# Another order of the convolution units, with the keys' lower half last, on one NeuronCore

## Chip, cores and metric

The kernel runs on 1 core of one Trainium2 chip. The metric is the device time of one execution in microseconds. The kernel before took 4063.36 us (median of 3 runs, 4057.63 to 4075.92). A change of 0.5% of that is 20 us.

## What is computed

An image of 64 x 64 positions with 256 channels goes through two layers. The first is a hybrid of convolutions and attention; the second is a bidirectional state-space scan and a mixture of experts. All is in float32. The change touches the first layer only as far as the attention's inputs (and one step of the layer norm inside the attention phase):

```python
qkv = concat([conv(xc, W1, 0), conv(xc, W3, 1), conv(xc, W5, 2)])   # q: 1x1, k: 3x3, v: 5x5
qkv = conv(qkv, Wdw, 1, groups=3 * c)                               # depthwise 3x3
q, k, v = split(qkv, 3); q, k = l2n(q), l2n(k)                      # per head and position
attn = softmax(einsum('bhnc,bhmc->bhnm', q, k) * temperature)       # 8 heads, 4096 positions
o = conv(einsum('bhnm,bhmc->bhnc', attn, v), Wproj, 0);  x = x + o
```

## The kernel before

**Units.** `conv_phase` cuts the three convolutions into 12 units `(kind, half, t)`: kind q, k or v; half 0 (upper) or 1 (lower) of the picture; t one of the two groups of 128 output channels. This text writes k00 for `("k", 0, 0)`, v01 for `("v", 0, 1)`, and so on. The 3x3 and 5x5 convolutions are done in Winograd form along the rows: a k unit has 6 jobs (points), a v unit has 8; a job is one accumulated product of transformed weights and transformed inputs in a PSUM bank (L465). A q unit is four plain 1x1 products (L457).

**Stages of a unit.** For k and v, `transform_out` combines the jobs' results in pairs on VectorE (`out_t`, `pad`, L289 and L286; one of a pair is first copied by ScalarE, L494) and writes the convolution's rows into one of two tiles `pad`, used in turn (`pads[n % 2]`). `sides` (ScalarE, L518, L519) fills the columns at the margins. Then `depthwise` makes the 3x3 depthwise convolution of `pad` in two pieces: a first tap on ScalarE (L557), one tap by ScalarE and an accumulating DMA (L562, L563), and 15 taps on VectorE (L570; 768 values a row for half 0, 1280 for half 1). Of v, the result is turned by TensorE (`turn`, L637, copied by ScalarE, L639) and stored to `vd`. Of q and k, three chunks of 512 positions at a time are normalised: squares on ScalarE (L600), sums on TensorE (L601), inverse root on ScalarE (L608 to L610), spread on TensorE (L615), product on VectorE (L289 `acc<-acc,ps`), for q a copy on ScalarE (L624), and a store (L628).

**Halves.** The depthwise convolution of the lower half needs 9 rows of the upper half; they are kept in `edge` tiles in SBUF, copied by ScalarE (L795, L757). k and v of the same t use one `edge` tile.

**Fills.** What the jobs need is also made on VectorE: `all_weights` transforms weights (v: 15 steps of about 1.9 us for each t) and sends them to DRAM, from which the SP queue loads them again (L443); `inputs` makes the transformed inputs of a kind and half (v: about 32 us). Nine `place` buffers hold these inputs. The list `fills` sets their order, `step_fill` takes the next step.

**Order.** Inside `tc.manual_schedule` each engine runs its instructions in the order in which the program emits them. While unit n's jobs run on TensorE, its groups call `step(main)` (output transform), `feed()` (jobs, as far as their weights and inputs have been emitted; at most 3 not yet used, 4 PSUM banks), `tick()` (due norm stages), `step(before)` (depthwise of unit n-1), `step_fill()`. So the order in the VectorE and TensorE queues is fixed at build time, and an engine whose next instruction must wait does nothing else.

```python
units = [("k", h, t) for h in range(2) for t in range(CT)]
units += [("q", 0, 0), ("v", 0, 0), ("q", 0, 1), ("v", 0, 1), ("q", 1, 0), ("v", 1, 0), ("q", 1, 1), ("v", 1, 1)]
```

**End of the phase.** Of the last unit (v11), 16 of 40 rows are made by TensorE: `diagonal` puts the nine taps on diagonals, `products` (L533) multiplies `pad` by them. `attention_phase` then loads q, keys and values (L935, L916, L917) into SBUF that the convolution phase used; these loads are queued on SP behind the end of that phase. Its first score product is L1048.

Of the kernel before, what the change touches and what calls it, by code (L numbers as in the profile page):

```python
# [24 lines left out]
P = 128  # L25
# [3 lines left out]
CT = C // P  # L29
# [32 lines left out]
def step(gen, n=1):  # L62

    for _ in range(n):
        if gen is None or next(gen, StopIteration) is StopIteration:
            return False
    return True
# [115 lines left out]
def conv_phase(cx, xT, w1, w3, w5, temp, qd, kd, vd, uk, uv):  # L183
# [13 lines left out]
    nc, tc = cx.nc, cx.tc  # L197
    HR = 32
    LAG = 24
    TX = W // 4  # L200
    with ExitStack() as ctx:
        one = ctx.enter_context(tc.tile_pool(name="a_one", bufs=1))
# [24 lines left out]
        for pad in pads:  # L227
# [2 lines left out]
        edges = {  # L230
            k: one.tile([P, 9, 4, TX], FP, name=f"edge{i}") for i, k in enumerate((0, 1, ("q", 0), ("q", 1)))
        }
        out_t = one.tile([P, 4 * N], FP, name="out_t")
        wq = one.tile([P, CT, C], FP, name="wq")
        for t in range(CT):
# [187 lines left out]

        units = [("k", h, t) for h in range(2) for t in range(CT)]
        units += [("q", 0, 0), ("v", 0, 0), ("q", 0, 1), ("v", 0, 1), ("q", 1, 0), ("v", 1, 0), ("q", 1, 1), ("v", 1, 1)]
        jobs = [
            (u, i) for u in units for i in (range(4) if u[0] == "q" else PTS[u[0]])
        ]  # L430
# [90 lines left out]
        spare = one.tile([P, (H - LAG) * W // 2], FP, name="spare")  # L521
        diag = spare[:, 0 : 9 * P].rearrange("p (a b) -> p a b", b=P)

        def diagonal(ch):
            for tap in range(9):
                w_ap = wdw[:, 9 * ch + tap : 9 * ch + tap + 1]
                nc.scalar.activation(diag[:, tap, :], cx.ident, AF.Copy, scale=w_ap)

        def products(pad, r, ps):

            for tap in range(9):
                dy, dx = divmod(tap, 3)
                nc.tensor.matmul(  # L533
                    ps.rearrange("p (h s j) -> p h s j", s=4, j=TX), diag[:, tap, :],
                    pad[:, r + dy : r + dy + 8, dx : dx + 4, :], start=tap == 0, stop=tap == 8,
                )

        def depthwise(kind, half, t, pad):

            row0, n = (LAG, H - LAG) if half else (0, LAG)  # L540
            ch = {"q": 0, "k": CT, "v": 2 * CT}[kind] + t
            dst = accp.tile([P, (H - LAG) * W], FP, name="acc", tag="acc")
            shared = 16 if (kind, half, t) == units[-1] else 0
            mine = n - shared

            def piece(b, tap):
                dy, dx = divmod(tap, 3)
                m = mine // 2
                return (
                    dst[:, m * W * b : m * W * (b + 1)].rearrange("p (h w) -> p h w", w=W),  # L550
                    pad[:, m * b + dy : m * b + dy + m, dx : dx + 4, :].rearrange("p h s j -> p h (s j)"),
                    wdw[:, 9 * ch + tap : 9 * ch + tap + 1],
                )

            for b in range(2):
                o, src, w_ap = piece(b, 0)
                nc.scalar.activation(o, src, AF.Copy, scale=w_ap)  # L557
            away = (kind, half, t) not in units[-2:]
            if away:
                o, src, w_ap = piece(1, 8)  # L560
                x = spare[:, 0 : mine * W // 2]
                nc.scalar.activation(x.rearrange("p (h w) -> p h w", w=W), src, AF.Copy, scale=w_ap)  # L562
                nc.gpsimd.dma_start(out=dst[:, mine * W // 2 : mine * W], in_=x, accum_op=ALU.add)  # L563
            parts = [pcv.tile([P, N], FP, name="cv", tag="cv") for _ in range(shared // 8)]
            for i, ps in enumerate(parts):
                products(pad, mine + 8 * i, ps)
            for b in range(2):
                for tap in range(1, 8 if b and away else 9):
                    o, src, w_ap = piece(b, tap)
                    nc.vector.scalar_tensor_tensor(o, src, w_ap, o, ALU.mult, ALU.add)  # L570
                    yield
                if kind == "v":
                    m = mine * W // P // 2
                    turn(dst, t, row0 * W // P, m * b, m)
                if b == 0 and shared:
                    for i, ps in enumerate(parts):
                        nc.scalar.copy(dst[:, W * (mine + 8 * i) : W * (mine + 8 * i + 8)], ps)
                    turn(dst, t, row0 * W // P, 2 * m, shared * W // P)
            if kind != "v":
                c0 = row0 // ROWS  # L580
                rows_left.extend((dst[:, N * j : N * j + N], kind, t, c0 + j) for j in range(n // ROWS))
                if not busy and (kind, half, t) == units[-2]:
                    norm_sums()
                elif not busy:
                    busy.append(None)
                    later(norm_sums)
# [68 lines left out]
        with tc.manual_schedule(engines=ORDERED):  # L655
# [56 lines left out]
            def all_weights(kind, co):  # L712
# [5 lines left out]
                ready.add((kind, co))  # L718

            fills = [  # L720
                first, all_weights("k", 1), inputs("k", 1),
                all_weights("v", 0), inputs("v", 0),
                all_weights("v", 1), inputs("v", 1),
            ]

            pure = fills[1::2]

            second = fills[5]

            def step_fill():  # L730

# [20 lines left out]
            before = None  # L752
            for n, (kind, half, t) in enumerate(units):
                pad, r0 = pads[n % 2], 9 if half else 1
                edge = edges[(kind, t) if kind == "q" else t]
                if half:
                    nc.scalar.copy(pad[:, 0:9, 1:5, :], edge)  # L757
                    nc.gpsimd.memset(pad[:, HR + 9, :, :], 0.0)
                else:
                    nc.gpsimd.memset(pad[:, 0, :, :], 0.0)  # L760
                if kind == "q":
                    def evacuate():
                        for i in range(4):
                            r = r0 + 16 * (i // 2)
                            nc.scalar.copy(
                                pad[:, r : r + 16, 1 + 2 * (i % 2) : 3 + 2 * (i % 2), :],
                                product().rearrange("p (h s j) -> p h s j", s=2, j=TX),
                            )
                        sides(pad, r0)
                        yield  # L770

                    main, groups = evacuate(), 1
                else:
                    main, groups = transform_out(kind, pad, r0), len(PTS[kind]) // 2
                if n == 0:
                    feed()
                    for _ in range(6):
                        step_fill()
                for g in range(groups):
                    step(main)  # L780
                    feed()
                    tick()

                    for _ in range(12 if kind == "q" else 0):
                        step_fill()

                    for _ in range(9 if n == len(units) - 1 else -(-18 // groups)):
                        step(before)
                    for _ in range(share[kind]):
                        step_fill()  # L790
                    feed()
                drain(main)
                drain(before)
                if not half:
                    nc.scalar.copy(edge, pad[:, LAG : LAG + 9, 1:5, :])  # L795
                before = depthwise(kind, half, t, pad)
                if n == len(units) - 2:
                    diagonal(2 * CT + units[-1][2])

            left = True  # L800
            while left or events:
                tick()
                for _ in range(4):
                    left = left and step(before)

# [79 lines left out]
def attention_phase(cx, early, xT, wproj, qd, kd, vd, x1d, ud):  # L887
# [8 lines left out]
    with ExitStack() as ctx:  # L896
# [41 lines left out]
        def project(c, oT):  # L938

            xr = tl.tile([P, CT, N], FP, name="xr", tag="xr")  # L940
            nc.sync.dma_start(out=xr, in_=xT[:, N * c : N * c + N].rearrange("(t p) n -> p t n", p=P))
            yield
            x1 = tl.tile([P, CT, N], FP, name="x1", tag="x1")
            for co in range(CT):
                ps = aside()
                for t in range(CT):
                    nc.tensor.matmul(
                        ps, wpj[:, t, P * co : P * co + P], oT[:, t, :], start=t == 0, stop=t == CT - 1
                    )
                yield  # L950
                nc.vector.tensor_tensor(x1[:, co, :], xr[:, co, :], ps, ALU.add)
                yield
            nc.sync.dma_start(out=x1d[c], in_=x1)
            if c == NCH - 1:
                return
            u = tl.tile([P, CT, N], FP, name="u", tag="xr")
            yield from layer_norm(cx, tl, aside, x1, u, None, 1, halves=True)
            nc.sync.dma_start(out=ud[c], in_=u)
            yield

# [1456 lines left out]
```

## Time and profile before

| | us |
|---|---|
| median of 3 runs (lowest, highest) | 4063.36 (4057.63, 4075.92) |
| the profiled execution | 4052.57, span 4050.8 |
| first convolution product on TensorE starts | 37.83 |
| first product of a v unit starts | 211.76 |
| last convolution product (L465) and the norm products after it end | 566.7 |
| q load of the attention issued on SP | 604.02 |
| first attention score product starts | 611.56 |

The profile comes from one execution. Engines: PE is TensorE, DVE is VectorE, ACT is ScalarE, POOL is GpSimd, SP issues DMAs. In a timeline a row is "start, duration, engine, line, operation, output<-input, shapes, count", and in brackets the idle time before it with what ended it; PE lists two entries for each product of the program. In the table by windows the columns are the window, its length, each engine's busy time with its count of instructions, the granted clock of TensorE, the DMA share and GB/s.

### The profile page before, as it was taken

What the parts mean: (1) busy time and instruction counts of PE and PEld (TensorE: products, weight loads), DVE (VectorE), ACT (ScalarE), POOL (GpSimd) and SP (SyncE); (2) the same over time, 40 slices, a digit from 0 to 9 for tenths busy, and PEclk for the clock granted to TensorE, in tenths of its full rate; (3) what the DMA queues carried; (4) which work ended last, traced back from release to release, by engine and by line L of the source; (5) the groups of instructions that cost most, each with busy time, mean ns of one, the idle gap of its engine ahead of it and who ended that gap; (6) DMA issues with size and microseconds to landing.
All of it is one profiled execution on the core that took longest, in us unless ns stands there. A gap on an engine that the chain in (4) does not pass through costs nothing. (4 is left out here: it accounts for less than half of the span.)

```text
span 4050.8 us, 43236 instructions
## 1 busy us (share of the span) xinstructions
PE 3566.8 (88%) x14792; PEld 1173.0 (29%) x14792; DVE 3441.4 (85%) x2887; ACT 2656.2 (66%) x4152; POOL 1849.2 (46%) x1294
## 2 busy tenths in 40 slices
PE   6789989999999999997888888888888888886898
PEld 2333432222222222222222222222222222222444
DVE  8997668988988888778899999999999999999322
ACT  1123238887887888775777777777787777775222
POOL 3120010000000000013888899898898989987100
PEclk9889989999999999998888898999899899988999
DMA  6342315232232332224343344243434444432111
GB/s 215 105 134 93 100 63 154 53 74 53 64 69 51 66 67 53 51 53 150 105 122 115 111 123 144 99 146 116 129 109 122 127 126 121 135 108 94 63 62 56
DMA packets 165763, 404.91 MB, mean 100 GB/s; under 512 B 37157, under 2 KB 46629, under 8 KB 165278
## 3 DMA queue, kind: packets, MB, share of 16 engines
q1 hardware_dynamic: 137166, 304.26, 24.3%
q0 software_dynamic: 26064, 89.42, 9.5%
q10 hardware_dynamic: 2304, 8.39, 0.6%
q8 instruction: 118, 1.93, 0.2%
q14 instruction: 111, 0.91, 0.1%
HBM read 268.17 MB, written 79.56 MB: 86 GB/s over the span
## 5 line engine op out<-in xcount | busy, mean ns | idle before, releaser
L1907 POOL TENSOR_TENSOR dbx<-dtxr,b 128x1024 f32<-128x1024 f32 x512 | 1202.8, 2359 | 190.5 <-DVE da L1920 89.8
L1055 ACT ACTIVATE e<-sc 128x1024 f32<-128x1024 f32 x1024 | 993.9, 1023 | 183.3 <-PE sc L1048 153.5
L1920 DVE TENSOR_TENSOR_SCAN da<-da,state,dbx 128x1024 f32<-128x1024 f32 x432 | 1014.1, 2347 | 20.2 <-POOL dbx L1907 6.3
L965 DVE TENSOR_TENSOR s<-s,e 128x1024 f32<-128x1024 f32 x768 | 880.2, 1219 | 17.6 <-ACT e L1055 17.0
L1897 ACT ACTIVATE da<-dtr,aneg 128x512 f32<-128x512 f32 x1024 | 708.1, 692 | 33.9 <-DMA dtr<-dtd 3.3
L1048 PE MATMUL sc<-q,kS 32*128 32x512 f32 x4096 | 650.3, 646 | 17.0 <-ACT e L1055 12.9
L1925 DVE TENSOR_TENSOR h<-da,c 128x1024 f32<-128x1024 f32 x432 | 529.2, 1225 | 33.2 <-DVE da L1920 1.4
L972 PE MATMUL av<-e,vT 128*32 128x512 f32 x4096 | 555.0, 608 | 0.3 <-ACT e L1055 0.3
L988 POOL DMA_DIRECT2D s<-s x94 | 81.5, 880 | 943.7 <-DVE s L965 850.3
L1960 PE MATMUL y<-h,sel 128*32 128x512 f32 x2048 | 372.2, 659 | 92.0 <-DVE h L1925 67.6
L465 PE MATMUL cv<-v,u 128*128 128x512 f32 x928 | 414.2, 607 | 42.6 <-DVE out_t L289 15.6
L1048 PEld LDWEIGHTS sc<-q,kS 32*128 32x128 f32 x4096 | 212.0, 184 | 458.6 <-issue 246.8
L1353 PE MATMUL mm<-u,win 128*128 128x512 f32 x464 | 245.3, 670 | 64.5 <-ACT z L1461 28.2
L1951 ACT COPY state<-da 128x2 f32<-128x2 f32 x431 | 68.8, 160 | 293.6 <-DVE h L1925 290.8
L570 DVE SCALAR_TENSOR_TENSOR acc<-pad,wdw_s,acc 128x768 f32<-128x768 f32 (+1 forms) x182 | 224.7, 1240 | 42.5 <-ACT acc L557 37.1
L465 PEld LDWEIGHTS cv<-v,u 128*128 128x128 f32 x928 | 179.5, 195 | 273.8 <-issue 226.7
L143 POOL TENSOR_TENSOR ln_few<-ln_few,minus_half 128x4 f32<-128x4 f32 x29 | 38.4, 1325 | 399.1 <-DMA ln_few<-ln_row 235.7
L1399 PE MATMUL mm<-xp,taps 128*128 128x512 f32 x480 | 213.3, 596 | 0.1
L965 DVE TENSOR_TENSOR s<-e 128x1024 f32<-128x1024 f32 x128 | 151.9, 1218 | 58.1 <-ACT e L1055 57.9
L1920 DVE TENSOR_TENSOR_SCAN h<-da,state,dbx 128x1024 f32<-128x1024 f32 x80 | 187.5, 2344 | 12.5 <-ACT state L1951 9.8
L972 PEld LDWEIGHTS av<-e,vT 128*32 128x32 f32 x4096 | 82.2, 108 | 397.7 <-issue 386.9
L1930 POOL TENSOR_TENSOR h<-h,c 128x1024 f32<-128x1024 f32 x80 | 188.4, 2355 | 1.0 <-ACT state L1951 1.0
(379 smaller groups left out, 3859.2 us busy)
## 6 DMA issues: line engine op xcount, KB each, us to landing
dtr<-dtd SPq DMA_DIRECT2D x128, 512.0 KB
dtxr<-dtd SPq DMA_DIRECT2D x128, 512.0 KB
s<-s POOLq DMA_DIRECT2D x94, 512.0 KB, 5.8
b<-bcd SPq DMA_DIRECT2D x64, 256.0 KB
c<-bcd SPq DMA_DIRECT2D x64, 256.0 KB
dtd<-dt SPq DMA_DIRECT2D x64, 256.0 KB
dtd<-few SPq DMA_DIRECT2D x64, 256.0 KB
u<-uv SPq DMA_DIRECT2D x24, 640.0 KB
```

The source lines that it names most:

```text
L465: nc.tensor.matmul(rows4(ps), u[:, dy, P * ci : P * ci + P], v[:, dy : dy + HR, ci, :], start=dy + ci == 0, stop=dy == k - 1 and ci == CT - 1,
L570: nc.vector.scalar_tensor_tensor(o, src, w_ap, o, ALU.mult, ALU.add)
L965: nc.vector.tensor_tensor(z, x, y, ALU.add)
L972: nc.tensor.matmul(g.av[32 * h : 32 * h + 32, :], vT[:, kb, P * t + 32 * h : P * t + 32 * h + 32], es[h // 2][:, h % 2, :], start=kb == 0, ...
L1048: nc.tensor.matmul(ps[h // 2][:, h % 2, :], kS[r, t, P * kb : P * kb + P], q_t[r, t, :], start=True, stop=True,)
L1055: nc.scalar.activation(e, ps[i], AF.Exp)
L1353: nc.tensor.matmul(ps, win[d][:, t, P * e : P * e + P], u[:, t, ::-1] if d else u[:, t, :], start=t == 0, stop=t == CT - 1,)
L1897: nc.scalar.activation(da[:, v, :], dts[i, e, j][0][:, v, :], AF.Exp, scale=aneg[i % 2][:, a : a + 1])
L1907: nc.gpsimd.tensor_tensor(u, dts[i, e, j][1], bcs[i, k][0][:, None, :].to_broadcast([P, 2, N]), ALU.mult)
L1920: nc.vector.tensor_tensor_scan(das[n].rearrange("p v n -> p (v n)"), da.rearrange("p v n -> p (v n)"), u.rearrange("p v n -> p (v n)"), st ...
L1925: nc.vector.tensor_tensor(h, da, bcs[i, k][1][:, None, :].to_broadcast([P, 2, N]), ALU.mult)
L1960: nc.tensor.matmul(ys[i, e][32 * j : 32 * j + 32, :], cx.sel, hs[n + j // 2][:, j % 2, :], start=False, stop=k == SQ - 1,)
```

## The change

The units come in another order: k00, k01, v00, q00, v01, q01, v10, q10, v11, q11, k10, k11. The fills follow: after the keys' weights come the values' weights and inputs, and the inputs for the keys' lower half are last. Since k and v are no longer finished one after the other, the 9 rows of k go through DRAM (`k_edges`, a store and a load on the SP queue for each t) instead of an `edge` tile. The last unit is now k11. Its 16 rows on TensorE are dealt out among the VectorE taps (`products` has become a generator), its first taps are emitted ahead of the due norm stages (`left = step(before)` before the loop), and in the last unit's groups after the first `feed()` and `tick()` are called once more. In the attention phase the layer norm of chunk 6 gets one more step of distance (`rest` 2).

```diff
+    SHARED = 1
+        k_edges = [cx.rows.tile([P, 9, 4, TX], FP, name=f"k_edge{t}", tag=f"k_edge{t}") for t in range(CT)]
...
-        units = [("k", h, t) for h in range(2) for t in range(CT)]
-        units += [("q", 0, 0), ("v", 0, 0), ("q", 0, 1), ("v", 0, 1), ("q", 1, 0), ("v", 1, 0), ("q", 1, 1), ("v", 1, 1)]
+        units = [
+            ("k", 0, 0), ("k", 0, 1), ("v", 0, 0), ("q", 0, 0), ("v", 0, 1), ("q", 0, 1),
+            ("v", 1, 0), ("q", 1, 0), ("v", 1, 1), ("q", 1, 1), ("k", 1, 0), ("k", 1, 1),
+        ]
...
                     pad[:, r + dy : r + dy + 8, dx : dx + 4, :], start=tap == 0, stop=tap == 8,
                 )
+                yield
...
-            shared = 16 if (kind, half, t) == units[-1] else 0
+            shared = 16 if (kind, half, t) in units[-SHARED:] else 0
-            away = (kind, half, t) not in units[-2:]
+            away = (kind, half, t) not in units[-SHARED - 1 :]
...
-            for i, ps in enumerate(parts):
-                products(pad, mine + 8 * i, ps)
+            beside = [products(pad, mine + 8 * i, ps) for i, ps in enumerate(parts)]
+            yield
             for b in range(2):
                 for tap in range(1, 8 if b and away else 9):
                     o, src, w_ap = piece(b, tap)
                     nc.vector.scalar_tensor_tensor(o, src, w_ap, o, ALU.mult, ALU.add)
+                    for _ in range(3 if beside else 0):
+                        if beside and not step(beside[0]):
+                            beside.pop(0)
                     yield
...
+                while beside:
+                    drain(beside.pop(0))
...
             fills = [
-                first, all_weights("k", 1), inputs("k", 1),
-                all_weights("v", 0), inputs("v", 0),
-                all_weights("v", 1), inputs("v", 1),
+                first, all_weights("k", 1), all_weights("v", 0), inputs("v", 0),
+                all_weights("v", 1), inputs("v", 1), inputs("k", 1),
             ]
-            pure = fills[1::2]
-            second = fills[5]
+            pure = [fills[1], fills[2], fills[4]]
+            second = fills[4]
...
                 if half:
-                    nc.scalar.copy(pad[:, 0:9, 1:5, :], edge)
+                    if kind == "k":
+                        nc.sync.dma_start(out=pad[:, 0:9, 1:5, :], in_=k_edges[t])
+                    else:
+                        nc.scalar.copy(pad[:, 0:9, 1:5, :], edge)
...
+                    if n == len(units) - 1 and g > 1:
+                        feed()
+                        tick()
...
-                if not half:
+                if kind == "k" and not half:
+                    nc.sync.dma_start(out=k_edges[t], in_=pad[:, LAG : LAG + 9, 1:5, :])
+                elif not half:
                     nc.scalar.copy(edge, pad[:, LAG : LAG + 9, 1:5, :])
...
-            left = True
+            left = step(before)
             while left or events:
-                tick()
                 for _ in range(4):
                     left = left and step(before)
+                tick()
...
-            yield from layer_norm(cx, tl, aside, x1, u, None, 1, halves=True)
+            yield from layer_norm(cx, tl, aside, x1, u, None, 2 if c == NCH - 2 else 1, halves=True)
```

More of the change, by code (lines that the diff above doesn't have):

```diff
@@ L522, in conv_phase, with diagonal @@
         diag = spare[:, 0 : 9 * P].rearrange("p (a b) -> p a b", b=P)
-        def diagonal(ch):
+        FIRST = {"q": 0, "k": CT, "v": 2 * CT}
+        def diagonal(unit):
+            ch = FIRST[unit[0]] + unit[2]
             for tap in range(9):
@@ L536, in products @@
                 )
+                yield
         def depthwise(kind, half, t, pad):
             row0, n = (LAG, H - LAG) if half else (0, LAG)
-            ch = {"q": 0, "k": CT, "v": 2 * CT}[kind] + t
+            ch = FIRST[kind] + t
             dst = accp.tile([P, (H - LAG) * W], FP, name="acc", tag="acc")
-            shared = 16 if (kind, half, t) == units[-1] else 0
+            shared = 16 if (kind, half, t) in units[-SHARED:] else 0
             mine = n - shared
@@ L570, in depthwise @@
                     nc.vector.scalar_tensor_tensor(o, src, w_ap, o, ALU.mult, ALU.add)
+                    for _ in range(3 if beside else 0):
+                        if beside and not step(beside[0]):
+                            beside.pop(0)
                     yield
+                m = mine * W // P // 2
                 if kind == "v":
-                    m = mine * W // P // 2
                     turn(dst, t, row0 * W // P, m * b, m)
+                while beside:
+                    drain(beside.pop(0))
                 if b == 0 and shared:
@@ L577, in depthwise @@
                         nc.scalar.copy(dst[:, W * (mine + 8 * i) : W * (mine + 8 * i + 8)], ps)
-                    turn(dst, t, row0 * W // P, 2 * m, shared * W // P)
+                    if kind == "v":
+                        turn(dst, t, row0 * W // P, 2 * m, shared * W // P)
             if kind != "v":
@@ L754, in conv_phase @@
                 pad, r0 = pads[n % 2], 9 if half else 1
-                edge = edges[(kind, t) if kind == "q" else t]
+                edge = edges[(kind, t) if kind == "q" else t] if kind != "k" else None
                 if half:
-                    nc.scalar.copy(pad[:, 0:9, 1:5, :], edge)
+                    if kind == "k":
+                        nc.sync.dma_start(out=pad[:, 0:9, 1:5, :], in_=k_edges[t])
+                    else:
+                        nc.scalar.copy(pad[:, 0:9, 1:5, :], edge)
                     nc.gpsimd.memset(pad[:, HR + 9, :, :], 0.0)
@@ L797, in conv_phase @@
                 if n == len(units) - 2:
-                    diagonal(2 * CT + units[-1][2])
-            left = True
+                    diagonal(units[n + (SHARED == 1)])
+                elif len(units) - SHARED <= n < len(units) - 2:
+                    diagonal(units[n])
+            left = step(before)
             while left or events:
-                tick()
                 for _ in range(4):
                     left = left and step(before)
+                tick()
 class Early:
```

## Prediction

> **What bounds the kernel now.** I read the busy times by windows first, then the timelines of PE, DVE, ACT and SP up to the first attention product. From that product on every engine's instructions stand in the same order in both built programs (the `rest` edit moves none), so the change counts by when the attention can begin.
>
> ```profile
> 113.00:205.00 92.00, 62.88 (x153) 25.89 (x152) 86.79 (x94) 19.80 (x29) 7.90 (x14) 0.85 0.30 92
> 205.00:310.00 105.00, 88.78 (x213) 37.07 (x214) 94.32 (x141) 25.04 (x39) 26.01 (x47) 0.91 0.43 139
> ...
> 480.00:567.00 87.00, 83.45 (x213) 35.85 (x211) 59.94 (x51) 28.83 (x47) 5.94 (x11) 0.98 0.23 76
> 567.00:612.00 45.00, 29.38 (x80) 12.27 (x84) 23.49 (x41) 19.67 (x30) 7.06 (x13) 0.75 0.26 84
> ```
>
> Up to 310 DVE is nearly full (86.79 of 92, 94.32 of 105) and PE waits; from 480 to 567 PE is full (83.45 of 87) and DVE has 27 free; the last 45 bind neither: there a chain runs through all engines.
>
> ```profile
> 126.81 18.45 PE L465 MATMUL cv<-v,u 128*128 128x512 f32 x36 [13.76 <-DVE pad L286]
> ...
> 205.65 6.27 PE L457 MATMUL cv<-xpad,wq 128*128 128x512 f32 x8 [16.00 <-DVE pad L286]
> ...
> 272.66 18.93 PE L465 MATMUL cv<-v,u 128*128 128x512 f32 x40 [15.57 <-DVE out_t L289]
> ...
> 538.47 17.43 PE L465 MATMUL cv<-v,u 128*128 128x512 f32 x40
> ```
>
> PE loses 45 in three waits for DVE. The rows also give prices: a v job (20 entries) takes 17.43/2 = 8.71, a k job (12) 5.2. After the first wait 36 entries take 18.45 where 36 x 0.436 = 15.7 would do, so a start costs 2.8 more (again 2.8 after the second wait, 1.5 after the third).
>
> ```profile
> 315.27 15.65 DVE L570 SCALAR_TENSOR_TENSOR acc<-pad,wdw_s,acc 128x768 f32<-128x768 f32 x15 [9.23 <-ACT acc L557]
> ...
> 490.17 23.72 DVE L570 SCALAR_TENSOR_TENSOR acc<-pad,wdw_s,acc 128x1280 f32<-128x1280 f32 x15 [10.96 <-ACT acc L557]
> ...
> 576.06 4.18 DVE L570 SCALAR_TENSOR_TENSOR acc<-pad,wdw_s,acc 128x768 f32<-128x768 f32 x4 [8.02 <-ACT acc L557]
> ```
>
> The 15 taps cost DVE 15.6 for an upper and 23.7 for a lower unit. q11's products ended on PE at 485.3 and the taps of the unit ahead of it began at 490.17: 4.8 through ACT. The last output was written at 566.4, the taps of the last unit began at 576.06: 9.7 through ACT's copies, squares and inverse roots.
>
> ```profile
> 604.02 0.83 SPq L935 DMA_DIRECT2D q<-qd  x2
> ```
> ```profile
> 611.56 5.39 PE L1048 MATMUL sc<-q,kS 32*128 32x512 f32 x16 [3.85 <-DMA kS<-kd]
> ```
>
> From SP's q load to the first scores it is 7.5.
>
> **The change, step by step.** I follow the new queues as built, with these prices, in the profiled execution's time; at each handover the later engine counts.
>
> Start of the values: DVE has finished the keys' weights at 60.8, as before. Ahead of v00's first input now stand 15 weight steps x 1.92 = 28.8, key outputs 9.7, 11 taps x 1.03 = 11.3, input rows 6.6, and a wait for raw weights (2.06 in the trace; 2.5 for the larger v load). Sum 58.9: v00 starts on PE at 119.7 (first v job before: 211.76). PE has been idle since the keys' twelve jobs ended at 102.
>
> v00 and q00: PE 2.8 + 8 x 8.71 + norm products 2.2, to 194.4; q00 7.0, to 201.4.
>
> The gap: next in PE's queue is v00's turn. v01's jobs stand behind it, since the last of v01's weights are emitted only during q00. The turn needs v00's taps. DVE's norm product waits for PE until 185.2; then 1.9, five taps 5.1, three weight steps 5.8, v00's last output and a tap 2.2: 200.2. Then 7 weight steps 13.4 with store waits of 2.5 (4.3 in 12 steps of the trace), and 15 taps 15.6: 231.7. With the rest of the turn PE begins v01 at 233.9, after some 25 of idling. DVE's next instruction is v01's first output; it needs a start and two jobs, 2.8 + 17.4 and a copy of 0.6, so DVE idles until 254.7. Each engine waits for the other in turn.
>
> PE leads again: v01 and q01 80.6, to 314.5; v10 and q10 with v01's turn 83.0, to 397.5; three jobs and a norm sum 27.2, to 424.7. v10's taps end at 397.5 + 4.8 + 23.7 = 426.0; half of its turn is then left, to 431.4; five jobs, a spread and q11 51.7, to 483.1.
>
> Keys' lower half: v11's taps end at 483.1 + 4.8 + 23.7 = 511.6. PE has run three k10 jobs and waits with v11's turn for these taps; half a turn 3.5, copies and k10's first output to 517.6. From here DVE is the bound: wait for ACT's first taps 2.0, q11's 15 taps 23.7, outputs of k10 and k11 6.0, products of two norm rounds 3.1: 552.4. ACT's q copies 2.0, squares 1.7 and first tap 1.3 come ahead of k10's taps: 557.4; 16 taps 25.3 and k11's outputs 4.8: 587.5. This point, the last output written, lay at 566.4: +21.
>
> The tail: 9.7 and a part of one more q copy, 10.2, to 597.7. DVE: 4 taps 4.2, products 1.9, 8 taps 8.3, to 612.1. The spread that it needs now stands behind PE's 18 tap products (16.8 in the trace, from 598.2) and a norm sum 1.1: 616.8, so DVE waits 4.7. Products 1.8, 4 taps 4.2: 622.8. Here the units differ in kind: v11 had only to be turned, beside the last taps; k11 must be normalised after them: squares 1.2, sums 0.7, ACT's three steps 2.1, spread 0.9 = 4.9, and a second round of 4.5. SP's q load comes at 632.4, the scores at 639.9. Before 611.56: +28.3, of which 21 up to the last output and 7 in the tail.
>
> At nothing: the key margins. Their stores wait on SP for the last outputs of k00 and k01 (about 80 and 131), ahead of v weights needed from 120 and 178 on. k10's load waits on SP for v11's taps (511.6), ahead of k11's weights, which PE needs from about 531; ACT needs the margins at 544. The trace has no such transfer; its nearest rows land in 2.5 (256 KB store) to 8.6 (384 KB raw weights). Either fits into the 19 up to 531; without that cover it costs 2.5 to 8.6. Behind k11's load are only the attention's loads. The four edge copies of 0.66 that ACT is spared lie beside other work.
>
> [...]
>
> Bounds: starts at 1.5 and no waits for loads and stores, -8; two more starts in the keys' phase, +6, and first key blocks landing behind five late key stores, +3. So +20 to +37. The profiled 4052.57 lies 10.8 under the median 4063.36. I add to the median: 4091.7, by the bounds 4083 to 4100; the three runs before lie up to 6 below and 13 above theirs.
>
> **Rivals.** (1) Faster: PE is the bound from 119.7 on. Its rows then sum to 2.8 + four pairs of 76.7 + keys 62.4 + norms 17.6 + turns 21.8: last product at 531, with the old tail of 45 scores at 576, -35: 4028. It holds as far as PE's waits after 119.7 stay under 35 in sum. For it, v starts 92 earlier; against it, the 25 at v00's turn, and DVE's queue from 487.9 on. (2) No difference: the gap stands, but DVE keeps up in the keys' phase, so that PE ends at about 561 and the scores start 45 + 7 later, at 613: +2, 4065. For it, DVE had 27 free in the last window; against it, three times 24 of lower taps now meet 62 of key jobs. (3) Worse than forecast: k10's margins hold back k11's weights, and the last key stores the first scores by 8: +45, 4108.
>
> **How the numbers follow.** Forecast 0.62, rivals 0.08, 0.20 and 0.10. Over 0.5% is over 20 us, about what a measurement of this kernel can tell from no change: slower = forecast and rival 3, 0.72; same = rival 2, 0.20; faster = rival 1, 0.08. The range leaves out rival 1 and part of rival 2: 4065 to 4108.
>
> **What would show it.** In the profile after: first v product near 120; PE idle until a turn near 225 and DVE idle some 20 directly after 232; v11's taps ending near 511; last `pad` output near 587; SP's q load near 632 and the first score near 640. I am wrong if the first score starts before 625, or if PE has no wait over 15 after 125.

## The result, and the profile after

The changed kernel takes 4107.80 us (median of 5 runs, 4094.59 to 4111.19), the kernel before on the same chip 4067.00 (median of 5, 4057.63 to 4075.92). The ratio is 1.0102, its 95% interval 1.0081 to 1.0122: slower by 41 us, where 28 were forecast. The profiled execution took 4103.91, its span is 4102.0; that of before lay 14 below its own median (4052.57 against 4067.00), so the two profiled spans differ by 51, more than the kernels do.

First the busy times by the same windows as before.

```profile
113.00:205.00 92.00, 79.90 (x188) 34.33 (x188) 83.27 (x116) 11.55 (x20) 12.88 (x22) 0.92 0.33 106
205.00:310.00 105.00, 78.99 (x190) 34.52 (x189) 69.98 (x92) 14.86 (x24) 14.55 (x27) 0.87 0.34 109
480.00:567.00 87.00, 73.08 (x184) 31.45 (x183) 67.42 (x57) 36.60 (x57) 8.28 (x16) 0.90 0.33 98
567.00:612.00 45.00, 20.34 (x50) 6.90 (x49) 35.52 (x34) 12.37 (x19) 1.62 (x3) 0.67 0.04 17
```

Up to 205 PE gains what the change is after: 79.90 busy instead of 62.88. The next window gives it back on both engines: DVE falls from 94.32 to 69.98 of 105 and PE from 88.78 to 78.99, neither is full. From 567 on DVE is the busy one (35.52 of 45), where before a chain through all engines was already ending the phase.

The timeline of PE names the handovers:

```profile
124.07 45.07 PE L469 MATMUL cv<-v,u 128*128 128x512 f32 x100 [21.83 <-DVE v L291]
...
225.24 1.11 PE L651 MATMUL tr<-ident,acc 128*128 128x128 f32 x4 [15.34 <-DVE acc L578]
...
234.67 1.09 PE L651 MATMUL tr<-ident,acc 128*128 128x128 f32 x4 [6.95 <-issue]
...
236.95 44.88 PE L469 MATMUL cv<-v,u 128*128 128x512 f32 x100
...
315.15 5.40 PE L461 MATMUL cv<-xpad,wq 128*128 128x512 f32 x8 [2.87 <-DVE pad L288]
...
487.56 3.70 PE L461 MATMUL cv<-xpad,wq 128*128 128x512 f32 x8 [2.64 <-DVE pad L288]
...
519.99 1.09 PE L651 MATMUL tr<-ident,acc 128*128 128x128 f32 x4 [7.29 <-issue]
...
607.79 12.09 PE L540 MATMUL cv<-pad,spare 128*128 128x512 f32 x22
...
656.12 5.32 PE L1071 MATMUL sc<-q,kS 32*128 32x512 f32 x16 [7.51 <-DMA kS<-kd]
```

The values start at 124, 88 earlier than before. Then PE waits 15.34 and 6.95 with v00's turn (L651) for the taps of v00, and v01's products start only behind it. (For the second wait the profile names no engine; the last seven taps of v00 run on DVE from 227.22 to 234.56, and the turn goes on at 234.67.) q01 and q11 wait for DVE at 315.15 and 487.56, and the second part of v11's turn waits 7.29. Of the tap products of the last unit (L540), the first 22 entries take 12.09. The first score starts at 656.12, 44.6 later than the 611.56 before. The timeline of DVE shows the other side, and the tail:

```profile
64.77 0.76 DVE L291 TENSOR_TENSOR wx<-wr 128x256 f32<-128x256 f32 x2 [4.66 <-DMA wr<-in_w]
...
84.43 0.76 DVE L291 TENSOR_TENSOR wx<-wr 128x256 f32<-128x256 f32 x2 [3.46 <-DMA wr<-in_w]
...
256.74 1.29 DVE L291 TENSOR_TENSOR out_t<-cv,c 128x512 f32<-128x512 f32 x2 [22.18 <-ACT c L498]
...
594.74 1.28 DVE L288 SCALAR_TENSOR_TENSOR pad<-cv,out_t 128x512 f32<-128x512 f32 x2
...
628.16 1.88 DVE L291 TENSOR_TENSOR acc<-acc,ps 128x512 f32<-128x512 f32 x3 [7.43 <-PE ps L629]
...
641.59 1.88 DVE L291 TENSOR_TENSOR acc<-acc,ps 128x512 f32<-128x512 f32 x3 [6.84 <-PE ps L629]
648.64 1.28 DVE L291 TENSOR_TENSOR acc<-acc,ps 128x512 f32<-128x512 f32 x2 [5.17 <-PE ps L629]
```

Waits for raw weights ahead of the values' start (64.77, 84.43), the idle of 22.18 behind v00's taps, the last output written at 596.0 (566.4 before), and behind the last taps two more rounds of norms, at 641.59 and 648.64, with only SP's q load (648.78) after them.

What follows the first score is not the change's: from there to the end of the span it is 3445.9 after and 3439.2 before, and 3438.7 to 3459.1 over all fourteen profiles of this study. So I compare kernels by medians, and phases by the first score. That is not free of scatter either. The changed kernel and three of those below (`a_lesstaps`, `a_nonorm`, `a_warm`) have the same code up to the second part of v11's turn, and it starts there at 519.99, 518.33, 519.73 and 525.03. A difference of less than 7 between the first scores of two single profiles therefore says little by itself. The stretch from this point to the first score says more: it is 136.1 in the changed kernel, and 135.9 and 136.2 in two kernels whose edits lie ahead of it (`a_fill`, `a_wr3`).

### The profile page after: what moved, and what is told of

It reads as the page before. It is cut to its first block, busy times and chain, and to the rows that moved or that the text cites. A ratio compares the mean times of both kernels' runs of the same rounds, so it can differ in the third digit from the quotient of the medians.

```text
span 4102.0 us, 43243 instructions
## 1 busy us (share of the span) xinstructions
PE 3573.0 (87%) x14792; PEld 1175.8 (29%) x14792; DVE 3445.6 (84%) x2887; ACT 2653.3 (65%) x4148; POOL 1849.6 (45%) x1294
## 5 line engine op out<-in xcount | busy, mean ns | idle before, releaser
L1943 DVE TENSOR_TENSOR_SCAN da<-da,state,dbx 128x1024 f32<-128x1024 f32 x432 | 1014.0, 2347 | 16.4 <-ACT da L1920 6.5
L1071 PE MATMUL sc<-q,kS 32*128 32x512 f32 x4096 | 650.5, 646 | 20.9 <-ACT e L1078 13.1
```

Of the source, the lines that this page charges most:

```text
L1071: nc.tensor.matmul(ps[h // 2][:, h % 2, :], kS[r, t, P * kb : P * kb + P], q_t[r, t, :], start=True, stop=True,)
L1943: nc.vector.tensor_tensor_scan(das[n].rearrange("p v n -> p (v n)"), da.rearrange("p v n -> p (v n)"), u.rearrange("p v n -> p (v n)"), st ...
```

## Experiments

My theory after the result: four losses one behind the other. (i) DVE starts the values late, since it waits for raw weights; (ii) PE and DVE wait for each other in turn at v00's turn; (iii) in the keys' lower half DVE is the bound; (iv) k11 has to be normalised behind its last taps, with PE at a granted clock of 0.50 (634 to 656). The rivals: the margins through DRAM, the dealt products of the last unit, and that the losses lie in parallel, so that taking one away uncovers another. Line numbers in the kernels below differ from the changed kernel's by a few.

**The new tail alone, in the kernel before** (`b_tail`): only the dealing of the products (with the `yield` ahead of the taps), the extra `feed()` and `tick()`, and the taps ahead of the norm stages.

```diff
-            for i, ps in enumerate(parts):
-                products(pad, mine + 8 * i, ps)
+            beside = [products(pad, mine + 8 * i, ps) for i, ps in enumerate(parts)]
+            yield
...
-            left = True
+            left = step(before)
...
```

> The kernel before with only the new handling of the last unit (its tap products dealt three to a tap, its taps begun at once, the extra feed and tick). Before, the first attention score started at 611.56, after a wait of DVE of 8.22 for a spread that stood behind 36 tap products. Theory (the loss of the change lies in the order of the units): the dealing shortens that wait a little, first score at 608 to 611, total within 5 us of before. Rival (the dealing itself delays the spreads): first score at 615 or later, total 4 us or more slower.

Measured: 4064.78 (median of 10 runs) against 4068.01 (20 runs), ratio 0.9994, interval 0.9981 to 1.0007. The first score came at 616.0, outside the 608 to 611. But q11's products, ahead of the last unit, already start at 482.35 instead of 478.31; from there to the first score it is 133.7, and 133.3 before. So the dealing itself costs nothing. Where the 4.0 ahead of it come from stays open: PE has the same order up to there, but the added `yield` in `depthwise` moves one VectorE tap of every unit a step later (the changed kernel has it too), and scatter is as large.

**The old tail in the changed kernel** (`a_oldtail`): the same edit the other way round.

> The changed kernel with only the old handling of its last unit (all 36 tap products at once, no extra feed and tick). Theory (order of the units): up to the last output written (596 in the changed kernel) nothing moves by more than 3; the wait for the spread at 628.16 grows by 1 to 4, first score at 657 to 661 instead of 656.12. Rival (the dealing is what made the tail 15 longer): first score at 652 or earlier.

Measured: first score at 660.05, one run of 4100.52; the last output moved by 1.9, DVE's wait for the spread is 8.36 instead of 7.43 and ends at 630.96 instead of 628.16. The score is 3.9 later, as the theory said, though the wait grew by 0.9 only. v11's turn is 0.5 later, so the old handling costs about 3 here, and the new one is no cause of the loss.

**v01's weights ahead of q00** (`a_fill`):

```diff
-                    for _ in range(share[kind]):
+                    for _ in range(7 if n == 2 else share[kind]):
```

> The changed kernel with 7 instead of 3 weight steps in each group of v00, so that all weights of v01 are made before q00 and v01's first three jobs stand in PE's queue ahead of v00's turn; all other orders are kept. Theory (in the gap PE and DVE waited for each other in turn): PE starts v01 by 224 instead of 236.95, DVE's idle of 22.18 at 256.74 shrinks to under 8, and 10 to 18 of it last to the end: first score at 638 to 646, total 10 to 18 below the changed kernel. Rival (DVE or PE is the bound anyhow and gives it back): first score at 652 or later.

Timelines of PE and DVE of this kernel:

```profile
213.61 6.29 PE L461 MATMUL cv<-xpad,wq 128*128 128x512 f32 x8 [11.81 <-DVE pad L288]
219.74 25.91 PE L469 MATMUL cv<-v,u 128*128 128x512 f32 x60
```
```profile
252.13 1.29 DVE L291 TENSOR_TENSOR out_t<-cv,c 128x512 f32<-128x512 f32 x2 [12.41 <-ACT c L498]
```

PE starts v01 at 219.74 instead of 236.95, and DVE's idle falls from 22.18 to 12.41, not under 8. First score at 644.29, 11.8 earlier; 4093.28 (median of 5), ratio to before 1.0060 (1.0039 to 1.0082). So loss (ii) is real. But the edit takes only about half of the idling away: PE's waits between v00's and v01's products fall from 27 to 14 (now 11.81 ahead of the last two products of q00, for DVE, whose weight steps come before v00's outputs), DVE's from 22 to 12. About 12 of that reached the end (11.8 by the first score, with v00 already 1.6 earlier, ahead of the edit; 14.5 by the medians). What the other half costs no run shows.

**A third buffer for raw weights** (`a_wr3`):

```diff
...
-            r = pool.tile([P, 5, C], FP, name="wr", tag=tag, bufs=2 if pool is rp else None)
+            r = pool.tile([P, 5, C], FP, name="wr", tag=tag, bufs=3 if pool is rp else None)
...
-            ahead = [load_raw(*pieces.pop(0))]
+            ahead = [load_raw(*pieces.pop(0)) for _ in range(2)]
```

> The changed kernel with a third buffer for raw weights, so that their loads start one piece earlier (the room is taken from the margins of q, which share the values' margin tiles here, so the margin rows of q10 and q11 hold the values' content). Theory (the late start of the values comes from DVE's waits for raw weights, 9.7 in four, of which the prediction allowed 2.5): the waits for wr between 55 and 240 fall to under 3, PE starts v00 at 116 to 120 instead of 124.07, and the first score comes 3 to 9 earlier, 647 to 653. Rival (the loads are bound by the transfers themselves, another buffer changes nothing): the waits stay at 7 or more, v00 at 123 or later.

DVE's waits between 55 and 240, summed by releaser (us in all, times, longest): first the changed kernel, then this one; last this one's first v product.

```profile
DVE wx L291 <- DMA wr<-in_w: 9.7, 4, 4.7
```
```profile
DVE wx L291 <- DMA wr<-in_w: 0.9, 1, 0.9
```
```profile
118.19 46.01 PE L469 MATMUL cv<-v,u 128*128 128x512 f32 x100 [13.62 <-DVE v L291]
```

Loss (i): 9.7 of waits become 0.9, and the values start 5.9 earlier, at 118.19 (the four profiles with the same code have 122.03 to 124.07). The first score comes at 649.26, 6.9 earlier; by itself that is no more than the scatter, but it fits what the values gained. The one run took 4103.64.

**Half of the taps of q11 and k10 left out** (`a_lesstaps`):

```diff
-                for tap in range(1, 8 if b and away else 9):
+                for tap in range(1, 5 if (kind, half, t) in units[-3:-1] else 8 if b and away else 9):
```

> The changed kernel with 8 of the 15 or 16 taps of q11 and of k10 on DVE (the others are left out), which spares DVE 15 x 1.58 = 23.7 between 525 and 595; PE's work is untouched. Theory (DVE is the bound of the keys' lower half): PE's last k11 product ends at 577 within 3 as in the changed kernel, the last output comes 12 to 17 earlier (579 to 584 instead of 596), and the first score at 639 to 645. Rival (PE or the weights' loads set the end of this phase): first score at 652 or later.

```profile
580.53 1.29 DVE L288 SCALAR_TENSOR_TENSOR pad<-cv,out_t 128x512 f32<-128x512 f32 x2
```

This is the last output on DVE: it ends at 581.8 instead of 596.0, while PE's last k11 product ended at 575.5 (its products up to there are untouched and without waits from 522 on). First score at 641.28, 14.8 earlier. Of that 1.7 stood ahead of the edit (v11's turn at 518.33); from v11's turn to the first score it is 13.2 less. The one run took 4095.50. Loss (iii): DVE sets the end of this phase. The 13 are what these taps cost there; with another number left out it would be another.

**k11 stored without its normalisation** (`a_nonorm`):

```diff
-            if kind != "v":
+            if (kind, half, t) == units[-1]:
+                for j in range(n // ROWS):
+                    nc.gpsimd.dma_start(out=kd[t][:, N * (row0 // ROWS + j) : N * (row0 // ROWS + j + 1)], in_=dst[:, N * j : N * j + N])
+            elif kind != "v":
```

> The changed kernel with the rows of k11, the last unit, stored as its taps leave them; the normalisation of these five chunks (1536 pixels by taps and products, two and a part rounds of squares, sums, inverse roots, spreads) is left out. Changed kernel: last tap ends at 634.1, first score at 656.12. Theory (the tail is longer since k11 is normalised behind its taps): last tap unmoved within 3, first score 641 to 647, so that the stretch from the last output written (596) to the first score is 45 to 50, as the 46 before. Rival (the tail's length lies in the spreads, loads and stores as such): first score at 652 or later.

```profile
642.89 5.32 PE L1074 MATMUL sc<-q,kS 32*128 32x512 f32 x16 [9.87 <-DMA kS<-kd]
```

13.2 earlier (13.0 from v11's turn on), and 47 from the last output to the first score, where the kernel before has 45. The one run took 4096.94. Loss (iv).

**Matmuls that keep PE's clock up** (`a_warm`): two, read by nobody, behind the sums of the last four rounds.

```diff
+            if tail:
+                x = pcv.tile([P, N], FP, name="cv", tag="cv")
+                for _ in range(2):
+                    nc.tensor.matmul(x, cx.ident, out_t[:, 0:N], start=True, stop=True)
...
+            tail.append(1)
```

> The changed kernel with two matmuls (into a free bank, read by nobody) behind the norm sums of each of the last four rounds, in the time in which PE waits for ACT's inverse roots. Theory (the last two rounds take 7.5 and 7.1 instead of the 4.9 and 4.5 priced because PE runs them at half speed after idling): the sums and spreads behind 634 take about half of the changed kernel's 2.40, 2.08, 1.92 and 2.07, and the stretch from the last tap's end (634.1) to the first score (656.1), 22.0, shrinks by 1 to 4. Rival (their length is ACT's and the semaphores', not PE's): durations and stretch stay within 0.5, or the stretch grows by the added matmuls.

First the last two spreads and the windows of the changed kernel (the figure behind the five busy times is the granted clock), then those of this one:

```profile
639.48 2.08 PE L629 MATMUL ps<-rn,pick 32*128 32x512 f32 x6 [2.19 <-ACT rn L624]
...
646.53 2.07 PE L629 MATMUL ps<-rn,pick 32*128 32x512 f32 x4 [2.19 <-ACT rn L624]
```
```profile
634.00:645.00 11.00, 6.41 (x16) 1.12 (x16) 2.62 (x5) 4.83 (x8) 2.16 (x4) 0.50 0.17 67
645.00:656.00 11.00, 2.07 (x4) 0.50 (x4) 4.23 (x17) 1.42 (x3) 1.15 (x2) 0.50 0.62 184
```
```profile
646.29 1.13 PE L633 MATMUL ps<-rn,pick 32*128 32x512 f32 x6
...
651.53 1.13 PE L633 MATMUL ps<-rn,pick 32*128 32x512 f32 x4 [0.28 <-ACT rn L628]
```
```profile
634.00:645.00 11.00, 8.31 (x22) 2.11 (x19) 6.46 (x8) 5.56 (x10) 2.17 (x4) 0.84 0.24 96
645.00:656.00 11.00, 6.52 (x22) 1.75 (x20) 5.19 (x16) 4.16 (x7) 2.78 (x5) 0.96 0.38 118
```

With the clock at 0.84 and 0.96 instead of 0.50 a spread takes 1.13 instead of 2.08, and the stretch from the last taps' end to the first score falls from 22.1 (634.06 to 656.12) to 19.1 (640.75 to 659.82). The first sum behind the taps stayed as slow (2.41, and 2.40 in the changed kernel). So PE's clock is about 3 of the tail's excess. Little of it is left as a whole: the first two added matmuls stand ahead of a spread and delay it (DVE waits 9.11 instead of 7.43 for it), and from v11's turn to the first score it is 134.8 instead of 136.1. The one run took 4115.20, 11 more than the profiled run of the changed kernel: 5.0 of that lie ahead of the edit (v11's turn at 525.03) and 7.7 behind the first score.

**No transfers of the keys' margins** (`a_nomargin`):

```diff
-                        nc.sync.dma_start(out=pad[:, 0:9, 1:5, :], in_=k_edges[t])
+                        nc.scalar.copy(pad[:, 0:9, 1:5, :], edges[t])
...
-                if kind == "k" and not half:
-                    nc.sync.dma_start(out=k_edges[t], in_=pad[:, LAG : LAG + 9, 1:5, :])
-                elif not half:
+                if kind != "k" and not half:
```

> The changed kernel without the transfers of the keys' margins: nothing is stored to DRAM, and the margin rows of k10 and k11 are filled by an ACT copy from the tiles of the values' margins (of that time's content), so two stores and two loads on SP are left out. Theory (they cost nothing): from the first k10 output (525) to the last output (596) the stretch keeps its 71 within 2, first score at 652 to 660. Rival (k10's margin load holds back k11's weights or ACT's side copies): that stretch 4 or more shorter.

First and last output of the keys' lower half on DVE:

```profile
528.74 1.29 DVE L291 TENSOR_TENSOR out_t<-cv,c 128x512 f32<-128x512 f32 x2 [6.01 <-ACT c L498]
...
598.59 1.28 DVE L288 SCALAR_TENSOR_TENSOR pad<-cv,out_t 128x512 f32<-128x512 f32 x2
```

The stretch is 71.1 (to 599.9) with the transfers left out and 70.7 (525.32 to 596.0) with them; v00 starts at 123.69, as in the others. The first score came at 660.21, just outside the 652 to 660, with 2.9 of its delay already at v11's turn (522.84); the one run took 4112.81. The margins cost nothing that these profiles show.

**The keys' lower half in the middle** (`a_kmid`, and `a_kmid2_fill` with a q unit between the value units and v01's weights early):

```diff
-            ("v", 1, 0), ("q", 1, 0), ("v", 1, 1), ("q", 1, 1), ("k", 1, 0), ("k", 1, 1),
+            ("k", 1, 0), ("k", 1, 1), ("v", 1, 0), ("q", 1, 0), ("q", 1, 1), ("v", 1, 1),
...
-                all_weights("v", 1), inputs("v", 1), inputs("k", 1),
+                all_weights("v", 1), inputs("k", 1), inputs("v", 1),
```

> The changed kernel with the keys' lower half moved between the values' two halves: k00, k01, v00, q00, v01, q01, k10, k11, v10, q10, q11, v11; margins through DRAM, the dealt products and the gap at v00's turn are kept, the last unit is v11 as before. Theory (besides the gap, the keys' lower half as the last pair costs, by DVE's taps there and by the normalisation of k11 behind its taps): first score at 605 to 625 instead of 656, total within 15 of the kernel before. Rival (the loss comes from the late start of the values, the gap and the margins, wherever the keys stand): first score at 640 or later.

> Units k00, k01, v00, q00, v01, q01, k10, k11, q10, v10, q11, v11, with the 7 weight steps in v00's groups: the keys' lower half in the middle, a q unit between any two of the last value units, last unit v11. Theory (the gap costs about 12, the two q units side by side in the run with k10 and k11 in the middle cost 11 to 18 at 487 and 499, the last pair the rest): first score at 597 to 608, total 3 to 15 below the kernel before. Rival (with DVE as the bound from 315 on nothing of it lasts): first score at 615 or later, total no better than before.

```profile
487.81 1.11 PE L651 MATMUL tr<-ident,acc 128*128 128x128 f32 x4 [11.41 <-DVE acc L578]
```
```profile
393.35 6.49 PE L461 MATMUL cv<-xpad,wq 128*128 128x512 f32 x8 [14.42 <-DVE pad L288]
```

`a_kmid`: first score at 628.51, 27.6 earlier than the changed kernel and 3.5 later than hoped; 4076.53 (median of 10), ratio 1.0016 (1.0004 to 1.0029). Two q units side by side leave PE waiting 11.41 for v10's taps (first line). `a_kmid2_fill` mends both this and the gap, and was to beat the kernel before; it did not: 615.28, 4065.73 (median of 10), ratio 0.9996 (0.9981 to 1.0010). Its new wait is the second line: behind k10 and k11, at 393, PE waits 14.42 for DVE. My expectation (597 to 608) fell, and its rival's numbers stood. The rival's reason, that DVE is the bound from 315 on, isn't shown: from 315 to 597 DVE is busy for 219.8 of 282 us here and PE for 249.8 (before: 200.1 and 265.2). What the run shows is that a wait taken away in one place came back in another.

**All four edits together** (`a_all`: `a_wr3`, `a_fill`, `a_lesstaps`, `a_nonorm`; the work that the last two leave out is left out here).

> The changed kernel with four of the single edits together: the third buffer for raw weights (6.9 earlier at the first score alone, q's margins sharing the values' tiles), 7 weight steps in v00's groups (11.8 alone), 8 instead of 15 or 16 taps for q11 and k10 (14.8 alone, taps left out) and k11's rows stored without their normalisation (13.2 alone, left out). Theory (four separate losses, one behind the other): the gains add up, 46.7 together, first score at 606 to 614, total within 10 of the kernel before. Rival (they are losses in parallel, and another wait takes over): first score at 622 or later.

```profile
506.93 1.09 PE L654 MATMUL tr<-ident,acc 128*128 128x128 f32 x4 [8.00 <-issue]
...
616.62 4.46 PE L1074 MATMUL sc<-q,kS 32*128 32x512 f32 x14 [8.86 <-DMA kd<-acc]
```

616.62: 39.5 earlier, where the single gains add up to 46.7 (606 to 614 were expected). From v11's turn to the first score it is 109.7 instead of 136.1, 26.4 less, and the single gains there are 13.2 and 13.0: (iii) and (iv) add up. Ahead of it, v01 starts at 214.50, 22.4 earlier, but the second part of v11's turn stands at 506.93 instead of 519.99, only 13.1 earlier; the edits alone had moved it by 11.6 (`a_fill`) and 6.9 (`a_wr3`). The 5 that are missing there can be an overlap of (i) and (ii), or scatter. The total, 4066.81 (median of 10), is that of before again (4070.28 from 13 runs, ratio 0.9995, 0.9980 to 1.0010). That the four make up just the 41 us isn't shown by it, since (iii) and (iv) went by leaving work out, which no order does.

**Less work on DVE, in the kernel before** (`b_pool`: `b_tail`, and six instructions of the values' input transform on POOL).

```diff
-                    plus(x, e, f)
-                    plus(f, e, f, ALU.subtract)
+                    g = nc.gpsimd if kind == "v" and half else nc.vector
+                    g.tensor_tensor(x, e, f, ALU.add)
+                    g.tensor_tensor(f, e, f, ALU.subtract)
...
-                plus(e, e, d[0], ALU.subtract)
-                plus(f, f, d[1], ALU.subtract)
+                nc.gpsimd.tensor_tensor(e, e, d[0], ALU.subtract)
+                nc.gpsimd.tensor_tensor(f, f, d[1], ALU.subtract)
```

> The kernel before with the new handling of the last unit and with six tensor_tensor instructions of the values' input transform moved from DVE to the idle POOL (the last two of each half, and two more of the lower half), which spares DVE 6 x 1.36 = 8.2. Theory (DVE's work is what bounds every order here up to the tail): first score 3 to 9 earlier than the 616.0 of the run with the new handling alone, total 0.1 to 0.25 per cent below the kernel before. Rival (the values' inputs come later from the slower POOL, and PE waits for that): first score at 615 or later, total no lower.

4062.21 (median of 12) against 4068.77 (17 runs), ratio 0.9980 (0.9969 to 0.9991): the lowest ratio of the study, though by 0.2% only, and its interval overlaps `b_tail`'s. The total is as the theory said, but the first score, 617.67, did not come earlier than `b_tail`'s 616.00, as the rival said. So the profile doesn't show the gain that the runs do; why it is faster stays open.

## Why the prediction was right and wrong

The direction and the path held: the first score came after 625, PE has a wait over 15 after 125 at the place named, DVE idles directly behind it, and DVE's taps set the keys' phase. The size failed: 28.3 was too little, against 44.6 in the profiled pair and 41 in the medians. (The forecast time, 4091.7, missed 4107.80 by 16; 4 of that is the median before, now 4067.00.) The step that failed most is the pricing of the tail, behind the last output. By the checkpoints of the walk:

| checkpoint | forecast | measured | late by |
|---|---|---|---|
| v00 starts on PE | 119.7 | 124.1 | 4.4 |
| v01 starts on PE | 233.9 | 237.0 | 3.1 |
| q11 ends on PE | 483.1 | 491.3 | 8.2 |
| last output written | 587.5 | 596.0 | 8.5 |
| last tap ends | 622.8 | 634.1 | 11.3 |
| SP's q load | 632.4 | 648.8 | 16.4 |
| first score | 639.9 | 656.1 | 16.2 |

- **Start of the values: mis-sized.** "a wait for raw weights (2.06 in the trace; 2.5 for the larger v load)" was one wait, and its row, at 58.42, was the keys'. In its place stand two, 4.66 and 3.46 (of four with 9.7 in all): with 15 value steps in a row DVE uses up a piece of 640 KB (three steps, 5.7 from 74.04 to 79.69) faster than two buffers let it come (7.4 from issue to landing, the median of five loads between 55 and 100). With a third (`a_wr3`) the values start 5.9 earlier.
- **The gap: right in size, place and sequence** (15.34 and 6.95 on PE, 22.18 on DVE, v01 within 3.1). It had no price of its own in the forecast; taking about half of it away (`a_fill`) brought 12.
- **PE's stretch from v01 to q11: mis-sized by 5.** Pairs were priced by PE's own rows. In the new order q01 and q11 wait 2.87 at 315.15 and 2.64 at 487.56 for DVE's last read of a bank (both `<-DVE pad`), which is about what the prices lacked.
- **The keys' lower half: right.** From q11's end to the last output 104.4 were forecast, 104.7 measured, and `a_lesstaps` shows the bound named.
- **The tail: the term that failed most,** by 7.9. The step "squares 1.2, sums 0.7, ACT's three steps 2.1, spread 0.9 = 4.9, and a second round of 4.5" priced PE's part below even the rows of the changed kernel at a granted clock of 1.00 (at 570.70 a round's sums take 1.06, at 577.03 its spread 1.13). The rounds took 7.5 and 7.1, 5.2 more in sum, at a granted clock of 0.50. With added matmuls (`a_warm`) they take 6.7 and 5.2, so about half of the 5.2 or more is the clock (the first sum stayed slow there); what else is in it stays open. The rows to use were a round of the kernel before in a stretch where PE idles (granted clock 0.50 from 570 to 578):

```profile
570.12 2.95 PE L601 MATMUL ps<-sq,heads 128*32 128x512 f32 x6 [3.40 <-ACT sq L600]
575.26 2.08 PE L615 MATMUL ps<-rn,pick_q 32*128 32x512 f32 x6 [2.19 <-ACT rn L610]
```

From its squares (569.45) to the end of its spread (577.34) it is 7.9. The other 2.7 that the tail lost are the wait for the spread, 7.43 instead of 4.7: the first 22 entries of the tap products took 12.09, where 0.436 each gives 9.6, at a granted clock of 0.67 from 606 to 616. (The terms given for that spread, 598.2, 16.8 and 1.1, add up to 616.1 and not to 616.8.)
- **The clock at the two starts** matters little: the granted clock was 0.51 from 124 to 128 and 1.00 from 128 to 132; the first 100 entries of v00 took 45.07, at 0.436 each 43.6, so the start lost 1.5, where I took 2.8; in `a_wr3` it lost 2.4 (46.01). At v01's start the clock was 0.50 from 236 to 240, and the 44.88 of its first 100 entries are a loss of 1.3. Where the clock matters is the tail, which I priced without it.
- **The margins: right at nothing** (71.1 without, 70.7 with the transfers in pieces of 256 B, which are hidden here; so what such pieces cost where they are not hidden, no run shows).
- **The rest edit** was in all kernels made from the changed one and was not run alone; the stretch behind the first score, 3445.9, lies within the 3439.2 to 3455.0 of the three kernels without it.

Of the rivals, the fast one fell at its own condition (PE's waits of over 1 us from v00's start to its last k11 product sum to 39.6, over the 35); the second fell because DVE did not keep up (`a_lesstaps`). The third, 4108, has the measured time by luck: the margins hold nothing back (`a_nomargin`), and from SP's q load to the first score it is 7.3 (before 7.5).

## What to carry over

In kernels whose queues are in order, price a new order by both queues at each handover, and do not add up what the two engines idle: here an edit that took 13 from PE's waits and 10 from DVE's brought about 12. Price a chain of small steps behind the last large work by rows from the same kind of place, with the granted clock of that place (0.50 in the tail here), not by rows of a full engine. Three orders here (before, `a_kmid`, `a_kmid2_fill`) lie within about 0.2% of each other although PE waits at other places in each: look where a wait that you take away can come back.

## Not expected of the hardware

The granted clock was 1.00 from 616 to 626, 0.94 from 626 to 634 and 0.50 from 634 to 656, and the forecast of the tail had no such fall in it. No idle gap of PE from 628 to 648 was longer than 2.2 us: in that time short bursts (1.0 to 2.4 us) stood between gaps of 0.86 to 2.2, and PE was busy for 6.41 of the 11 us from 634 to 645; with two added matmuls a round (`a_warm`) it was busy for 8.31 in the same window, and the clock was 0.84. Beyond this pair no run shows what the clock goes by.

Fourteen profiles whose instructions behind the first score are the same (but for the rest edit) scatter there by 20 us (3438.7 to 3459.1), and four with the same code ahead of v11's turn scatter there by 6.7. Part of that can be the clock: in the changed kernel 40 entries of products took 17.33 at 351.06 and 18.71 at 435.76, at a granted clock of 1.00 (351 to 355) and 0.57 (435.76 to 439), and of the 20 runs of the kernel before that stand beside `b_tail` the shortest (4056.67) had a mean granted clock of 0.934, the longest (4081.53) 0.927. A single pair of profiles would have put this change at 51 us instead of 41.
